# Where the nodes' scores of a four-layer graph network are computed, and when its projection runs: the scores move from TensorE to GpSimd and VectorE, the projection to another place, and one set of transposes becomes products with the identity

## The chip, the cores and the metric

The kernel runs on one core of a Trainium2 chip. The metric is the device time of one execution in microseconds (us), 1385.76 as the median of 14 runs before the change. The core has five engines that work side by side and wait for each other through semaphores: TensorE (PE, with its weight loads shown as PEld), VectorE (DVE), ScalarE (ACT), GpSimd (POOL) and SyncE (SP), which here issues nearly all DMAs. SBUF is the working memory of 128 partitions; PSUM is the small memory that matmuls write to.

## The reference, cut to what matters

x has 8 batches, 2048 nodes and 64 features. Four layers follow, each with a residual and a layer norm. Layer 0 weighs three terms of each node by the node's own weights; the second and third are products with the adjacency, A x and (2 A A - 1) x. Layer 1 projects the result and gives each node two scores per batch:

```python
    w = jnp.einsum('nd,dkio->nkio', embedding, weight)          # layer 0
    x_g = jnp.einsum('knm,bmc->bnkc', A_stack, x)
    out = jnp.einsum('bnki,nkio->bno', x_g, w)
    ...
    h = x @ W                                                   # layer 1
    s = jax.nn.leaky_relu(h @ a_node, 0.2)
    alpha = jax.nn.softmax(jnp.where(H.T > 0, s[:, None, :], NEG), axis=-1)
    agg = jnp.einsum('ben,bnf->bef', alpha, h)
    beta = jax.nn.sigmoid((h @ a_gn)[:, None, :] + (agg @ a_ge)[:, :, None])
    ...
    industry = jnp.einsum('nm,bmf->bnf', adj / deg, x @ W_ind)
```

The rest of layer 1 mixes `agg`, `h` and `industry`; layers 2 and 3 are products with the adjacency and with small weights. The change touches only how layer 0's term A x is brought into transposed form, and how and when `h`, the two scores `h @ a_node` and `h @ a_gn`, and `agg` are made.

## The kernel before, in words

The 2048 nodes are 16 tiles of 128 nodes (`NT` = 16), a tile holding 8 batches x 64 features = 512 columns. The stages are:

1. `first_product` (to about 149 us) makes y1 = A x for all tiles and keeps it as the sum of two parts, `y_hi` and `y_lo`, that TensorE can read in its rounded float32 form (fp32r).
2. `layer0` (about 150 to 743 us) is a loop over blocks j, one for each tile, and an extra round j = 16. This is where the change lies.
3. `layer1` (to about 1070 us), then layers 2 and 3.

A block of `layer0` has eight groups g = 0 to 7. In each, `weigh(j, g)` writes products of the three terms with the weights into a PSUM tile `pp` (L1020), 24 matmul instructions, and DVE adds four slices of it into the residual `r` (L1031). The PSUM pool of `pp` has two buffers. Between the groups other work of neighbouring tiles is placed, by hand: inside `program_order()` each of PE, DVE, ACT and POOL executes in exactly the order in which the Python code issues instructions, so a waiting instruction holds up all that stand behind it on its engine. SP's queue is in order too, but is arranged by the framework. The pieces that matter here:

- `first_terms(j+1)` after group 2: POOL adds `y_hi` and `y_lo` into `y1` (L956), PE transposes it (L152, named `try`), ACT copies the result to `y1T`; then the bias `bp`, and POOL prepares the next residual `r` (L969).
- `product(j+1)` after group 3: y2 = A y1 for the next tile, 32 matmuls of 512 columns (L983, `y2p`). `second_term(j+1)` after group 6: y2 transposed and finished on DVE (`y2T`, L999).
- `normed(j-1, ...)` after groups 0, 1, 2: layer norm of the tile before, ending in `x1`; `to_features(j-1)` after `product`: four transposes (`trx`), and ACT's copy `xT1`.
- `scores(j-1)` after group 6: PE multiplies `xT1` by `wa` (W times a_node and a_gn, made at the start), the tile `sgp` (L1077); ACT copies one half to `sg` and the other to `hgr`; DVE and ACT make `es` = exp(leaky_relu(score)).
- `project(j-1)` after group 7: PE multiplies `xT1` by both projections (`hp`, L1098), in a buffer of the same pool as `pp`; ACT copies `ihi` (or `y_hi`, L1115) and `h` (L1116), DVE makes `ilo` (L1117), two DMAs store `kept_i`; POOL makes `md` and `hs` = h times `es` (L1124).
- `gather(j-2)` after group 6: `aggp` accumulates `md` x `hs` (L1129).
- Masks: `mask(j+2)` (DVE, L927) from the adjacency loads, `scaled(j+1)` (POOL: `ms` L935 and sums `cs`), `compare(j+1)` (DVE, L948), `degrees(j+1)` (PE, `dgp`).

In the extra round j = 16, `gather(14)`, the sums of `es` (`denominators`, L1144), `scores(15)`, `project(15)` and `gather(15)` remain. `layer1` begins with `aggp`.

Of the kernel before, what the change touches and what calls it, by code (L numbers as in the profile page):

```python
# [8 lines left out]
F32 = mybir.dt.float32  # L9
# [9 lines left out]
P = 128  # L19
# [32 lines left out]
def kernel(  # L52
# [31 lines left out]

    ident = const.tile([P, P], F32, tag="ident", name="ident")
    make_identity(nc, ident)
    ones = const.tile([P, P], F32, tag="ones", name="ones")
    nc.vector.memset(ones, 1.0)
    eps_t = const.tile([P, 1], F32, tag="eps", name="eps_t")
# [17 lines left out]
    def b_view(t2):  # L107
        return t2.rearrange("p (b c) -> p b c", b=B)
# [771 lines left out]
    def layer0(  # L880
# [3 lines left out]

        h_sb, wb, wa, vecs, av_sb, pm, es, hgr, aggp, rden = layer1s
        raws, msk, terms, resid, norm, srow = {}, {}, {}, {}, {}, {}
        x1s, xTs, hps, hss, mds = {}, {}, {}, {}, {}

        homes = {"xT": (0, 1, 2), "xs": (3, 4), "y1": (5,), "y1T": (6, 7), "r": (8, 9),
                 "y2": (10,), "y2T": (11, 12), "cs": (13, 14), "sq": (15,)}
        turn = {}

# [7 lines left out]
        def load_adj(j):  # L902
            raws[j] = []
            for h in range(2):
                raw = rawp.tile([P, 8, P], F32, tag="raw", name=f"adj_{j}_{h}")
                for k in range(2):
                    nc.sync.dma_start(
                        raw[:, 4 * k:4 * k + 4, :],
                        at[j // 4, 2 * h + k][:, :, (j % 4) * P:(j % 4 + 1) * P],
                    )  # L910
                raws[j].append(raw)
            srow[j] = tile("srow", f"srow_{j}", (P, P), 3)
            nc.sync.dma_start(srow[j], s_row[0, j * P:(j + 1) * P].partition_broadcast(P))

        def load_x(j):
# [36 lines left out]

        def first_terms(j):

            y1 = tile("y1", f"y1_{j}")
            nc.gpsimd.tensor_tensor(y1, y_hi[:, j, :], y_lo[:, j, :], ALU.add)  # L956
            tr = ps_tr.tile([P, NP, P], F32, tag="tr", name=f"try1_{j}")
            for pr in range(NP):
                transpose(tr[:, pr, :], y1[:, pr * P:(pr + 1) * P])
            y1T = tile("y1T", f"y1T_{j}", (P, NP, P))  # L960
            nc.scalar.copy(y1T, tr)
            terms[j]["y1"] = y1T
            bp = ps_tr.tile([P, QW], F32, tag="tr", name=f"bp_{j}")
            nc.tensor.matmul(bp[:, 0:C], terms[j]["et"], bias_sb, start=True, stop=True)
            bn = tile("bn", f"bn_{j}", (P, C))
            nc.scalar.copy(bn, bp[:, 0:C])
            r = tile("r", f"r0_{j}")
            for bq in range(2):
                nc.gpsimd.tensor_tensor(  # L969
                    r[:, 4 * bq * C:4 * (bq + 1) * C]  # L970
                    .rearrange("p (h l c) -> p h l c", h=2, l=2),
                    swapped(terms[j]["xs"], bq),
                    bn.rearrange("p (h l c) -> p h l c", h=1, l=1).to_broadcast([P, 2, 2, C]),
                    ALU.add,
                )
            resid[j] = r
# [95 lines left out]
            nc.scalar.copy(xTs[j], tr)  # L1072

        def scores(j):
            sp = ps_tr.tile([P, NP, 2, 2], F32, tag="tr", name=f"sgp_{j}")
            for pr in range(NP):
                nc.tensor.matmul(  # L1077
                    sp[:, pr].rearrange("p i h -> p (i h)"), xTs[j][:, pr, :],
                    wa.rearrange("p i h -> p (i h)"), start=True, stop=True,
                )  # L1080
            sg = tile("sg", f"sg_{j}", (P, NP, 2))
            nc.scalar.copy(sg, sp[:, :, 0, :])
            nc.scalar.copy(hgr[:, j, 0, :].rearrange("p (r h) -> p r h", h=2), sp[:, :, 1, :])
            ej = es[:, j, :]
            nc.vector.scalar_tensor_tensor(
                ej.rearrange("p (r h) -> p r h", h=2), sg, 0.2, sg, op0=ALU.mult, op1=ALU.max
            )
            nc.vector.tensor_scalar(ej, ej, TOP, None, op0=ALU.min)
            nc.scalar.activation(ej, ej, AF.Exp)

        def project(j):

            mm = ps_p.tile([P, 2, 2, 4 * C], F32, tag="pp", name=f"hp_{j}")
            mm = mm.rearrange("p h l (m x) -> p h (l m) x", m=2)
            for pr in range(NP):
                for h in range(2):
                    rs = slice(h * 64, (h + 1) * 64)
                    nc.tensor.matmul(  # L1098
                        mm[:, h, pr, :], xTs[j][rs, pr, :], wb[rs], start=True, stop=True
                    )  # L1100
            if j < NT - 1:
                md = tile("md", f"md_{j}", (P, 2, E))
                nc.gpsimd.tensor_copy(md, pm[:, j, :].unsqueeze(1).to_broadcast([P, 2, E]))
                mds[j] = md.rearrange("p h e -> p (h e)")

            def by_half(t):
                return t.rearrange("p (r h c) -> p h r c", h=2, c=C)


            stay = j >= len(kept_i)  # L1110
            if stay:
                hi, lo = y_hi[:, j, :], y_lo[:, j, :]
            else:
                hi, lo = (tile(k, f"{k}_{j}", bufs=1) for k in ("ihi", "ilo"))
            nc.scalar.copy(r_(by_half(hi)), mm[:, :, :, C:2 * C])  # L1115
            nc.scalar.copy(by_half(h_sb[:, j, :]), mm[:, :, :, 0:C])  # L1116
            nc.vector.tensor_tensor(  # L1117
                r_(by_half(lo)), mm[:, :, :, C:2 * C], by_half(hi), ALU.subtract
            )
            if not stay:  # L1120
                for t, kept_part in zip((hi, lo), kept_i[j]):
                    nc.sync.dma_start(kept_part, t)
            hss[j] = tile("hs", f"hs_{j}", bufs=1)
            nc.gpsimd.tensor_tensor(  # L1124
                b_view(hss[j]), b_view(h_sb[:, j, :]), bcast(es[:, j, :]), ALU.mult
            )

        def gather(j):
            nc.tensor.matmul(aggp, mds[j], hss[j], start=j == 0, stop=j == NT - 1)  # L1129
# [1 line left out]
        def spread():  # L1131

            mds.clear()
            for q, home in enumerate((1, 2, 3, 5)):
                md = own.tile([P, 4, 2, E], F32, tag=f"b0_{home}", name=f"md4_{q}")
                nc.gpsimd.tensor_copy(
                    md, pm[:, 4 * q:4 * q + 4].unsqueeze(2).to_broadcast([P, 4, 2, E])
# [28 lines left out]
        with program_order():  # L1166
# [6 lines left out]
            for j in range(NT + 1):  # L1173
# [4 lines left out]
                for g in range(8):  # L1178
# [7 lines left out]
                    elif g == 1:  # L1186
                        when(j - 1, normed, 1)
                        if j == NT:
                            denp.append(ps_acc.tile([P, BC], F32, tag="acc", name="denp")[:, 0:B])
                            gather(NT - 2)  # L1190
                            spread()
                            denominators(0, NT - 1)
                        if first:
                            degrees(0)
                        when(j + 1, scaled, 0)
                    elif g == 2:
                        when(j - 1, normed, 2)
                        when(j + 1, first_terms)
                    elif g == 3:
                        if j + 1 < NT:  # L1200
                            for _ in product(j + 1):
                                pass
# [8 lines left out]
                        when(j + 2, mask, 1)  # L1211
                    elif g == 5:
                        when(j + 1, compare, 1)
                        if j:
                            next(flags, None)
                    elif g == 6:
                        when(j + 1, second_term)
                        when(j - 1, scores)
                        if j < NT:
                            when(j - 2, gather)  # L1220
                        else:
                            denominators(NT - 1, NT)
                            nc.vector.tensor_scalar(rden, denp[0], TINY, None, op0=ALU.max)
                            nc.vector.reciprocal(rden, rden)
                    elif g == 7:
                        when(j + 1, degrees)
                        when(j - 1, project)
            gather(NT - 1)


    def short_program(top):
# [7 lines left out]


        wb = wts.tile([P, 2 * C], F32, tag="wb", name="wb")
        wa = wts.tile([P, 2, 2], F32, tag="wa", name="wa")
        vecs = wts.tile([P, 3, C], F32, tag="vecs", name="vecs")
        pm = wts.tile([P, NT, E], F32, tag="pm", name="pm")
        es = wts.tile([P, NT, B], F32, tag="es", name="es")
# [4 lines left out]
        def load_weights():  # L1250
# [8 lines left out]
            block_diag(w2_sb[:, 1, :], w2n)  # L1259
            nc.sync.dma_start(bias2_sb, bias2.partition_broadcast(P))  # L1260
            block_diag(w3_sb, w3t)
            nc.gpsimd.memset(wa, 0.0)
            prod = wts.tile([P, C], F32, tag="prod", name="prod")
            for h in range(2):
                s = slice(h * 64, (h + 1) * 64)
                for i in range(2):
                    nc.vector.tensor_tensor(prod[s], wb[s, 0:C], vecs[s, i, :], ALU.mult)
                    nc.vector.tensor_reduce(wa[s, i, h:h + 1], prod[s], AX.X, ALU.add)

        def prepare(ps, pre):  # L1270
            for h in range(2):
# [27 lines left out]
        with tc.tile_pool(name="l0", bufs=1) as l0, tc.tile_pool(  # L1299
# [14 lines left out]
            with tc.tile_pool(name="l0s", bufs=2) as l0s, tc.tile_pool(  # L1314
# [3 lines left out]
            ) as ps_p:  # L1318
                layer0(
                    own, l0s, rawp, mskp, ps_acc, ps_tr, ps_p, w_sb, emb_sb, bias_sb, bad, deg,  # L1320
                    y_hi, y_lo, (h_sb, wb, wa, vecs, av_sb, pm, es, hgr, aggp, rden),
                )
                s1, dinv = cols_of["s1"], cols_of["dinv"]
                nc.vector.tensor_tensor(deg, deg, s1, ALU.mult)
# [717 lines left out]
```

## Time and profile before

| | before |
|---|---|
| median of 14 runs (lowest, highest) | 1385.76 us (1383.41, 1386.6) |
| the profiled execution: its own time | 1386.87 us |
| its span in the profile | 1384.8 us |
| mean TensorE clock granted | 0.96 of full |
| PE busy | 1308.0 us, 94% of the span |
| DVE busy | 929.3 us, 67% |
| ACT busy | 363.8 us, 26% |
| POOL busy | 442.5 us, 32% |

A row of the profile's groups names the source line, the engine, the operation, what it writes and reads with the shapes, and how often; then the busy time in us, the mean duration of one in ns, and the idle time of the engine just before such instructions, with what ended it. A row of a timeline begins with the start (us from the span's start) and the duration of the run of like instructions. Matmuls overlap in the pipeline, so what an instruction costs PE is read from one start to the next, not from its duration. The name behind an arrow in brackets is what the profile takes to have ended the wait; where that had long been done, it was another.

### The profile page before, as it was taken

How to read it: one execution, taken by the hardware profiler on the slowest of the kernel's cores; microseconds unless marked ns; L12 is line 12 of the kernel's file. 1: busy time of each engine (PE TensorE's matmuls, PEld its weight loads, DVE VectorE, ACT ScalarE, POOL GpSimd, SP SyncE). 2: the span in 40 equal slices, each digit the busy share in tenths (PEclk: the TensorE clock that was granted, in tenths of full speed). 3: DMA queues.
4: the chain of work that ended last, by engine and by line, in shares of the span. 5: the costliest groups of instructions: out<-in, count | busy, mean ns of one | idle time of the engine just before them, and what ended most of it. 6: DMA issues, size and time to landing. Idle time of an engine off the chain costs nothing.

```text
span 1384.8 us, 19824 instructions
## 1 busy us (share of the span) xinstructions
PE 1308.0 (94%) x7692; PEld 1025.3 (74%) x7692; DVE 929.3 (67%) x1658; ACT 363.8 (26%) x844; POOL 442.5 (32%) x372
## 2 busy tenths in 40 slices
PE   7999889999999999999986799999997899999997
PEld 6777678888888888888875466666665688888885
DVE  4555347787777777777672678888885666566554
ACT  3000101111112111111121346665655321111111
POOL 0000443444444444444410345665653320000000
PEclk9999989999999999999995699999999899999999
DMA  9765333333223332321503122222220223333552
GB/s 309 215 185 171 126 98 102 102 102 101 97 93 100 102 102 100 99 98 62 220 24 114 61 79 75 76 77 76 77 76 1 92 75 115 115 122 137 187 185 71
DMA packets 91047, 153.00 MB, mean 110 GB/s; under 512 B 12097, under 2 KB 55489, under 8 KB 84673
## 3 DMA queue, kind: packets, MB, share of 16 engines
q1 hardware_dynamic: 88642, 147.46, 31.7%
q10 hardware_dynamic: 2304, 4.20, 0.8%
q8 instruction: 63, 1.03, 0.3%
q14 instruction: 38, 0.31, 0.1%
HBM read 115.97 MB, written 35.66 MB: 110 GB/s over the span
## 4 chain that ended last, share of the span: by engine, by line
PE 91%; DVE 4%; issue 2%; ACT 1%; POOL 1%; DMA 1%; SPq 0%; POOLq 0%; ACTq 0%; DVEq 0%
PE pp L1020 24%; PE a L1288 17%; PE ind L1288 9%; PE y2p L983 9%; PE y1p L469 9%; PE fc L798 2%; PE u L1371 2%; PE df L807 2%; PE gp L693 2%; PE try L152 1%; PE yp L1400 1%; PE aggp L1129 1%; PE trm L152 1%; PE tr_l L152 1%; DVE r L1031 1%
## 5 line engine op out<-in xcount | busy, mean ns | idle before, releaser
L1031 DVE SCALAR_TENSOR_TENSOR r<-pp,emb_sb,r 128x256 f32<-128x256 f32 x512 | 247.1, 483 | 134.4 <-PE pp L1020 119.8
L1020 PE MATMUL pp<-w_sb,xT 64*128 64x256 f32 x1024 | 163.1, 391 | 11.7 <-PE hp L1098 10.3
L1020 PE MATMUL pp<-w_sb,y2T 64*128 64x256 f32 x1024 | 156.6, 378 | 0.0
L1020 PE MATMUL pp<-w_sb,y1T 64*128 64x256 f32 x1024 | 156.6, 378 | 0.0
L1020 PEld LDWEIGHTS pp<-w_sb,xT 64*128 64x128 f32 x1024 | 98.2, 187 | 34.6 <-issue 15.1
L469 PE MATMUL y1p<-x_hi,m 128*128 128x512 f32 x256 | 106.3, 415 | 7.3 <-ACT x_hi L417 7.2
L734 POOL TENSOR_TENSOR ez<-ez,coef 128x1024 f32<-128x1024 f32 x32 | 65.0, 2032 | 141.1 <-DVE ez L732 141.1
L1020 PEld LDWEIGHTS pp<-w_sb,y1T 64*128 64x128 f32 x1024 | 104.1, 188 | 7.8
L1020 PEld LDWEIGHTS pp<-w_sb,y2T 64*128 64x128 f32 x1024 | 104.1, 188 | 7.9
L1288 PE MATMUL ind<-y_hi,mj_l 128*128 128x512 f32 x256 | 106.6, 416 | 0.9 <-DVE dlt L763 0.8
L983 PE MATMUL y2p<-y_hi,msk 128*128 128x512 f32 x256 | 103.7, 405 | 0.0
L1288 PE MATMUL a<-y_hi,mj_l 128*128 128x512 f32 x256 | 102.4, 400 | 0.0
L469 PE MATMUL y1p<-x_lo,m 128*128 128x512 f32 x256 | 101.6, 397 | 0.0
L1288 PE MATMUL a<-y_lo,mj_l 128*128 128x512 f32 x256 | 101.6, 397 | 0.0
L983 PE MATMUL y2p<-y_lo,msk 128*128 128x512 f32 x256 | 101.6, 397 | 0.0
L1288 PE MATMUL ind<-y_lo,mj_l 128*128 128x512 f32 x256 | 101.0, 394 | 0.0
L1288 PE MATMUL a<-v_hi,mj_l 128*128 128x512 f32 x256 | 100.1, 392 | 0.0
L1288 PE MATMUL a<-v_lo,mj_l 128*128 128x512 f32 x256 | 100.0, 391 | 0.0
L1124 POOL TENSOR_TENSOR hs<-h,es 128x512 f32<-128x512 f32 x16 | 16.7, 1043 | 246.4 <-ACT h L1116 222.4
L935 POOL TENSOR_TENSOR ms<-msk,srow 128x1024 f32<-128x1024 f32 x32 | 77.4, 2419 | 7.5 <-DVE ms L948 5.2
L1288 PEld LDWEIGHTS ind<-y_hi,mj_l 128*128 128x128 f32 x256 | 48.6, 190 | 33.6 <-issue 19.1
L948 DVE SCALAR_TENSOR_TENSOR ms<-ms,adj 128x1024 f32<-128x1024 f32 x32 | 63.8, 1996 | 0.0
(262 smaller groups left out, 2433.3 us busy)
## 6 DMA issues: line engine op xcount, KB each, us to landing
mj_l<-mask SPq DMA_DIRECT2D x48, 1024.0 KB, 4.9
raw<-in_at SPq DMA_DIRECT2D x32, 512.0 KB, 4.9
adj<-in_at SPq DMA_DIRECT2D x64, 256.0 KB, 3.3
mask<-msk SPq DMA_DIRECT2D x32, 512.0 KB, 3.1
xraw<-in_xn SPq DMA_DIRECT2D x8, 512.0 KB, 5.5
oh<-oh SPq DMA_DIRECT2D x16, 256.0 KB, 4.1
xT<-in_xt SPq DMA_DIRECT2D x16, 256.0 KB, 2.9
xs<-in_xn SPq DMA_DIRECT2D x16, 256.0 KB, 2.5
```

Source lines behind the costliest of these rows:

```text
L152: nc.tensor.matmul(dst, src, ident, start=True, stop=True, is_transpose=True)
L469: nc.tensor.matmul(accs[q][jj], r_(m[:, t, jj * P:(jj + 1) * P]), r_(part[:, mt, :]), start=i + h + t == 0 and part is x_hi, stop=i == 3 a ...
L693: nc.tensor.matmul(gp[:, u, :], r_((oh01, oh23)[i][rs, cols]), r_(part[rs]), start=part is agg_hi, stop=part is agg_lo,)
L734: nc.gpsimd.tensor_tensor(by_b(ez), by_b(ez), per_b(coef, 2 * i, 2), ALU.mult)
L798: nc.tensor.matmul(fc[:, h, :], fcw_sb[rs], sT[rs], start=True, stop=True)
L807: nc.tensor.matmul(df[:, b:b + 1], th[:, b % 2, (b // 2) * P:(b // 2 + 1) * P], av_sb, start=True, stop=True,)
L935: nc.gpsimd.tensor_tensor(ms, m, srow[j].unsqueeze(1).to_broadcast([P, 8, P]), ALU.mult)
L948: nc.vector.scalar_tensor_tensor(ms, ms, 1.0, raws[j][h], op0=ALU.mult, op1=ALU.not_equal, accum_out=bad[:, 2 * j + h:2 * j + h + 1],)
L983: nc.tensor.matmul(acc, r_(msk[j, mt // 8][:, mt % 8, :]), r_(part[:, mt, :]), start=mt == 0 and part is y_hi, stop=mt == NT - 1 and part ...
L1020: nc.tensor.matmul(pp[:, h, pl, :], terms[j][name][rs, 2 * bq + pl], w_sb[rs, k, dq * 4 * C:(dq + 1) * 4 * C], start=k == 0, stop=k == K - 1,)
L1031: nc.vector.scalar_tensor_tensor(rb, ppv[:, :, dd, :], emb_sb[:, j, d:d + 1], rb, op0=ALU.mult, op1=ALU.add)
L1288: nc.tensor.matmul(acc, r_(a[:, mt, :]), r_(part[:, mt, :]), start=mt == 0 and part is hi, stop=mt == NT - 1 and part is lo,)
```

## The change

Three things, all in `layer0`, and what follows from them:

- `scores` uses no matmul any more. In `project`, POOL multiplies `h` by a_node and by a_gn into `hs` and a new tile `hm`; `scores` sums each over the features on DVE; a new `scale_h` on POOL then overwrites `hs` with `h` times `es`. `wa` and its making disappear.
- The order: `project(j-2)` stands after group 3, ahead of `product(j+1)`; `scores(j-2)` after group 5; `scale_h(j-2)` after group 6; `gather(j-2)` after group 7, behind `degrees`. In the extra round the last two tiles are finished one after the other.
- `first_terms` makes y1's transposed form by eight fp32r matmuls with an fp32r copy of the identity, `y_hi` and `y_lo` accumulating in PSUM; POOL's sum of the two disappears.

`srow` has two buffers in place of three.

```diff
@@ setup
+    ident_r = const.tile([P, P], F32, tag="ident_r", name="ident_r")
+    nc.vector.tensor_copy(r_(ident_r), ident)
@@ layer0
-        homes = {"xT": (0, 1, 2), "xs": (3, 4), "y1": (5,), "y1T": (6, 7), "r": (8, 9),
+        homes = {"xT": (0, 1, 2), "xs": (3, 4), "hs": (5,), "y1T": (6, 7), "r": (8, 9),
                  "y2": (10,), "y2T": (11, 12), "cs": (13, 14), "sq": (15,)}
...
-            srow[j] = tile("srow", f"srow_{j}", (P, P), 3)
+            srow[j] = tile("srow", f"srow_{j}", (P, P))
...
         def first_terms(j):
-            y1 = tile("y1", f"y1_{j}")
-            nc.gpsimd.tensor_tensor(y1, y_hi[:, j, :], y_lo[:, j, :], ALU.add)
             tr = ps_tr.tile([P, NP, P], F32, tag="tr", name=f"try1_{j}")
             for pr in range(NP):
-                transpose(tr[:, pr, :], y1[:, pr * P:(pr + 1) * P])
+                for part in (y_hi, y_lo):
+                    nc.tensor.matmul(
+                        tr[:, pr, :], r_(part[:, j, pr * P:(pr + 1) * P]), r_(ident_r),
+                        start=part is y_hi, stop=part is y_lo,
+                    )
...
         def scores(j):
-            sp = ps_tr.tile([P, NP, 2, 2], F32, tag="tr", name=f"sgp_{j}")
-            for pr in range(NP):
-                nc.tensor.matmul(
-                    sp[:, pr].rearrange("p i h -> p (i h)"), xTs[j][:, pr, :],
-                    wa.rearrange("p i h -> p (i h)"), start=True, stop=True,
-                )
-            sg = tile("sg", f"sg_{j}", (P, NP, 2))
-            nc.scalar.copy(sg, sp[:, :, 0, :])
-            nc.scalar.copy(hgr[:, j, 0, :].rearrange("p (r h) -> p r h", h=2), sp[:, :, 1, :])
             ej = es[:, j, :]
-            nc.vector.scalar_tensor_tensor(
-                ej.rearrange("p (r h) -> p r h", h=2), sg, 0.2, sg, op0=ALU.mult, op1=ALU.max
-            )
+            sg = tile("sg", f"sg_{j}", (P, B))
+            nc.vector.tensor_reduce(sg, b_view(hss[j]), AX.X, ALU.add)
+            nc.vector.scalar_tensor_tensor(ej, sg, 0.2, sg, op0=ALU.mult, op1=ALU.max)
             nc.vector.tensor_scalar(ej, ej, TOP, None, op0=ALU.min)
             nc.scalar.activation(ej, ej, AF.Exp)
+            nc.vector.tensor_reduce(hgr[:, j, 0, :], b_view(hms[j]), AX.X, ALU.add)
+
+        def scale_h(j):
+            nc.gpsimd.tensor_tensor(
+                b_view(hss[j]), b_view(h_sb[:, j, :]), bcast(es[:, j, :]), ALU.mult
+            )
...
         def project(j):
...
-            hss[j] = tile("hs", f"hs_{j}", bufs=1)
-            nc.gpsimd.tensor_tensor(
-                b_view(hss[j]), b_view(h_sb[:, j, :]), bcast(es[:, j, :]), ALU.mult
-            )
+            hss[j], hms[j] = (tile(k, f"{k}_{j}", bufs=1) for k in ("hs", "hm"))
+            for i, t in enumerate((hss[j], hms[j])):
+                nc.gpsimd.tensor_tensor(
+                    b_view(t), b_view(h_sb[:, j, :]),
+                    vecs[:, i, :].unsqueeze(1).to_broadcast([P, B, C]), ALU.mult,
+                )
...
                     elif g == 1:
                         when(j - 1, normed, 1)
                         if j == NT:
...
-                            gather(NT - 2)
                             spread()
-                            denominators(0, NT - 1)
+                            denominators(0, NT - 2)
...
                     elif g == 3:
+                        when(j - 2, project)
                         if j + 1 < NT:
                             for _ in product(j + 1):
                                 pass
...
                     elif g == 5:
                         when(j + 1, compare, 1)
+                        when(j - 2, scores)
...
                     elif g == 6:
                         when(j + 1, second_term)
-                        when(j - 1, scores)
+                        when(j - 2, scale_h)
+                    elif g == 7:
+                        when(j + 1, degrees)
                         if j < NT:
                             when(j - 2, gather)
-                        else:
-                            denominators(NT - 1, NT)
-                            nc.vector.tensor_scalar(rden, denp[0], TINY, None, op0=ALU.max)
-                            nc.vector.reciprocal(rden, rden)
-                    elif g == 7:
-                        when(j + 1, degrees)
-                        when(j - 1, project)
+            denominators(NT - 2, NT - 1)
+            gather(NT - 2)
+            project(NT - 1)
+            scores(NT - 1)
+            scale_h(NT - 1)
+            denominators(NT - 1, NT)
+            nc.vector.tensor_scalar(rden, denp[0], TINY, None, op0=ALU.max)
+            nc.vector.reciprocal(rden, rden)
             gather(NT - 1)
@@ short_program: wa, and the products and sums that made it at the start, are removed
```

More of the change, by code (lines that the diff above doesn't have):

```diff
@@ L883, in layer0 @@
     ):
-        h_sb, wb, wa, vecs, av_sb, pm, es, hgr, aggp, rden = layer1s
+        h_sb, wb, vecs, av_sb, pm, es, hgr, aggp, rden = layer1s
         raws, msk, terms, resid, norm, srow = {}, {}, {}, {}, {}, {}
-        x1s, xTs, hps, hss, mds = {}, {}, {}, {}, {}
-        homes = {"xT": (0, 1, 2), "xs": (3, 4), "y1": (5,), "y1T": (6, 7), "r": (8, 9),
+        x1s, xTs, hms, hss, mds = {}, {}, {}, {}, {}
+        homes = {"xT": (0, 1, 2), "xs": (3, 4), "hs": (5,), "y1T": (6, 7), "r": (8, 9),
                  "y2": (10,), "y2T": (11, 12), "cs": (13, 14), "sq": (15,)}
@@ L1100, in project @@
                     )
-            if j < NT - 1:
+            if j not in mds:
                 md = tile("md", f"md_{j}", (P, 2, E))
@@ L1133, in spread @@
             mds.clear()
-            for q, home in enumerate((1, 2, 3, 5)):
+            for q, home in enumerate((1, 2, 3, 10)):
                 md = own.tile([P, 4, 2, E], F32, tag=f"b0_{home}", name=f"md4_{q}")
@@ L1241, in short_program @@
         wb = wts.tile([P, 2 * C], F32, tag="wb", name="wb")
-        wa = wts.tile([P, 2, 2], F32, tag="wa", name="wa")
         vecs = wts.tile([P, 3, C], F32, tag="vecs", name="vecs")
@@ L1261, in load_weights @@
             block_diag(w3_sb, w3t)
[L1262 to L1268, printed above, removed]
         def prepare(ps, pre):
@@ L1320, in short_program @@
                     own, l0s, rawp, mskp, ps_acc, ps_tr, ps_p, w_sb, emb_sb, bias_sb, bad, deg,
-                    y_hi, y_lo, (h_sb, wb, wa, vecs, av_sb, pm, es, hgr, aggp, rden),
+                    y_hi, y_lo, (h_sb, wb, vecs, av_sb, pm, es, hgr, aggp, rden),
                 )
```

## The prediction

> **What bounds the kernel now.** I read the page first (engine shares, chain), then the waits of the layer-0 stretch, then one block of 128 nodes on each engine's timeline, then the two ends of the stage.
>
> ```profile
> PE 1308.0 (94%) x7692; PEld 1025.3 (74%) x7692; DVE 929.3 (67%) x1658; ACT 363.8 (26%) x844; POOL 442.5 (32%) x372
> ...
> PE 91%; DVE 4%; issue 2%; ACT 1%; POOL 1%; DMA 1%; SPq 0%; POOLq 0%; ACTq 0%; DVEq 0%
> ...
> L1020 PE MATMUL pp<-w_sb,xT 64*128 64x256 f32 x1024 | 163.1, 391 | 11.7 <-PE hp L1098 10.3
> ```
>
> The chain that ended last is PE in 91% of its length, so what PE is given to do, or waits for, is paid. Layer 0 runs from 150 to 743 us in blocks of 35.1 us; in the window 531.5 to 566.6 PE is busy 34.31 us, DVE 26.57, POOL 15.91, ACT 6.92. The idle column of the third line holds the only regular PE wait: 10.3 us, in 13 blocks. The PE timeline of that block, from y2's transposes to the next block's first group:
>
> ```profile
> 547.41 0.66 PE L152 MATMUL try<-ident,y 128*128 128x128 f32 x4
> 547.90 0.95 PE L1077 MATMUL sgp<-wa,xT 128*128 128x4 f32 x8
> 548.71 1.10 PE L1129 MATMUL aggp<-hs,md 128*128 128x512 f32 x2
> 549.75 0.70 PE L1020 MATMUL pp<-w_sb,xT 64*128 64x256 f32 x4
> ...
> 552.85 1.16 PE L1098 MATMUL hp<-wb,xT 64*128 64x128 f32 x16
> 554.80 0.70 PE L1020 MATMUL pp<-w_sb,xT 64*128 64x256 f32 x4 [0.79 <-PE hp L1098]
> ```
>
> Read start to start: the scores' eight products hold PE 547.90 to 548.71, **0.81 us**; the projection holds it 552.85 to 554.80, **1.95 us**, the last 0.79 idle. That wait is named PE hp, but hp had long ended. The next group needs a PSUM buffer of the pair that the group before hp filled, and DVE empties that one only at 554.7 (its last `r` instructions run 552.66 to 554.70). One extra user of the pair, with too little PE work behind it, makes the wait.
>
> The second place is block 0. PE timeline, then GpSimd's:
>
> ```profile
> 172.04 0.60 PE L1020 MATMUL pp<-w_sb,y2T 64*128 64x256 f32 x4
> 177.42 1.11 PE L152 MATMUL try<-ident,y 128*128 128x128 f32 x4 [4.79 <-POOL y L956]
> 178.47 0.68 PE L964 MATMUL bp<-bias_sb,et 16*128 16x64 f32 x2
> 179.08 1.23 PE L1020 MATMUL pp<-w_sb,xT 64*128 64x256 f32 x4
> ```
>
> ```profile
> 170.33 3.27 POOL L935 TENSOR_TENSOR ms<-msk,srow 128x1024 f32<-128x1024 f32 x1 [5.25 <-DVE ms L948]
> ...
> 176.11 1.26 POOL L956 TENSOR_TENSOR y<-y_hi,y_lo 128x512 f32<-128x512 f32 x1
> ```
>
> y1's sum waits on GpSimd behind the mask products, and those for a DVE compare: PE stands still 4.79 us. The group after it takes 5.42 us (179.08 to 184.50) where it normally takes 2.60, since the clock was granted at half.
>
> [...] after the 4.79 us, rows of 0.60 take 1.06. [...] sgp's eight matmuls have only 4 columns each, so loads set their pace, and they start every 0.10 us (0.81 / 8). [...] compare (L948) takes 2.94 us at 533.54 beside a GpSimd product, 1.14 us at 546.89 alone.
>
> **The change part by part**, in blocks whose order on each engine I read from the two programs.
>
> *Scores off PE.* sgp goes: -0.81 in 15 blocks = **-12.2**. The work returns elsewhere: two GpSimd products per block (the nearest row, he<-agg,vecs, took 1.26; so 2.5), less y1's sum (1.27); on DVE two reductions of 128x512 (0.68 as s_l) = 1.4; ACT loses two copies (0.17 each). Covers: GpSimd 15.9+1.25 of 34, DVE 26.6+1.4 = 28 of 34, so neither total binds; the order is looked at below.
>
> *Projection before y2's product.* hp (about 1.05 of PE) stays, but behind it stand 7.5 us of y2p and a transpose, in which DVE empties the buffer. So -(1.95-1.05) = -0.90 in about 14 blocks = **-12.6**. In block 15 there is no y2p: +0.5 there. Its evacuation (two ACT copies, DVE's ilo 0.69) and compare and masks (2.9 each) follow group 3 on DVE: done about 9.0 us after group 3, and group 4 ends at 11.9, so 2.9 us stay spare. The two `kept_i` stores move ahead of `srow` and adj loads on SP's queue; they wait for ilo, ready at +3.1, while srow waits for GpSimd's mask product (about +7) anyway, and the loads are for the next block's masks. On GpSimd the two products wait for ACT's h (about +2.4) and hold the mask product behind them to about +7.5; who waits for that is compare at group 5, at +16.5. The third srow buffer goes: its load then waits for a product that SP already waited for. Both at nothing; without that cover a load would be up to 4 us late against some 20 us of slack.
>
> *y1 by identity products.* Four transposes (527.73 to 528.32, 0.59, and 0.1 of wait on GpSimd's y) become eight fp32r products with a full weight load each. No such run exists in the trace. From below: the lone fp32r product of 128 columns, sm (L390), lets the next matmul start 0.06 us later: 8 x 0.06 = 0.48, a gain of 0.1. From above: 0.228 as for 512 columns, 1.82, a loss of 1.2. I take sgp's load pace [...] so with edges +0.3 in 16 blocks = **+4.8** (ends -1.6 and +19). Block 0's wait disappears, and with it the half clock: -4.79 - (5.42-2.60) = **-7.6**. Late next there: the y2 product's masks, ready since 151, so nothing.
>
> *The chain that the new scores hang on.* From the start S of DVE's group 5: group 1.96, compare 1.14, reduction 0.71, two small steps 0.36, Exp 0.3 (table loaded early, ACT is free), scale_h on GpSimd 1.04: done at S+5.55. PE comes to gather, now after degrees, at S-0.2 + groups 6 and 7 (5.3) + y2's transposes 0.5 + 0.3 = S+5.9. So gather waits for nothing, with **0.4 us to spare**; behind it stand all next groups. Group 6 leaves DVE at S+6.9, PE needs its buffer at S+7.0 after gather (1.04); group 7 at 9.4 against 9.6. Tight, and DVE is then level with PE until group 3 (DVE could end at S+20.2, PE's group 3 ends at S+18.7 and its DVE part at +20.7). I add 0.1 per block for brushes: **+1.5**.
>
> *The end of layer 0.* Before, from the last group at 719.84 to the last gather's end at 742.69: 22.9 us. After, in order: gather 13 and 28 denominators to +6.7, hp 14 to +8.7 (half clock, as hp at 736.24 took 2.08), trx; ACT h +10.0, GpSimd product +11.1, reduction, two steps, Exp +12.5, scale_h +13.6, gather 14 +15.7, hp 15 +17.8, h +19.0, product +20.1, reduction to Exp +21.5, scale_h +22.6, gather +24.7. With the products at 1.26, +25.1: **+2** (0 if the clock stays whole, +4 if the waits stretch).
>
> The ident_r copy on DVE lies in the 3.8 us that it waits for the first load; the removed weight products for `wa` are some small DVE steps. Nothing.
>
> Sum: -12.2 -12.6 +0.5 +4.8 -7.6 +1.5 +2 = **-23.6 us**. The profiled execution took 1386.87 (span 1384.8 and 2.1 around it), so 1363.3; it stood 1.1 above the median of 1385.76, so **1362.2**.
>
> **Rivals.**
> - *fp32r products at the price of 512 columns* (1.82 a block): -23.6 + 14.7 = -9, **1377**. For: no run of them in the trace. Against: sm's 0.06.
> - *The gather chain is late* (ends slower). It decides from 0.4 us on, then 1:1 on PE, 14 times. If compare at group 5 runs in its 2.94 us form (GpSimd's two extra products push its mask work beside it) and scale_h doubles beside DVE, the chain is 2.8 late: 2.4 x 14 = 34, and DVE's level stretch after it adds about 0.5 x 14 = 7: +17, **1403**. With compare alone slow: 1.4 x 14 = 20, **1382**. Against: GpSimd's mask work should end 11.7 us after group 3, compare comes at 16.5.
> - *The gain is absorbed*: DVE's level stretch stalls PE 1.4 us a block, and only block 0's part, the end and little else remain: **1382 to 1385**. Against: each buffer check above is met.
>
> **How the numbers follow.** Forecast 0.80 (own range 1355 to 1371: fp32r price down to 0.06, end 0 to +4, brushes 0 to 0.4 a block), fp32r dear 0.08, chain late 0.07 (0.05 of it slower), absorbed 0.05 (half under 1383). A run of this kernel tells apart some 0.2%, 2.8 us. Faster 0.91, same 0.03, slower 0.06. Range 1354 to 1378: it takes in the dear products and leaves out the late chain, the absorbed gain and the tails of the forecast, together under 2 in 10.
>
> **What would show it.** Right: no PE wait named hp; the y1 products in place of the try wait near 172 us, and pp at 0.60 behind them; blocks of about 33.7 us; PE aggp without idle time; last gather some 2 us later after the last group. Wrong: PE aggp waiting for POOL hs, pp waiting for DVE r in groups 0 to 2, y1 products starting 0.2 us apart, or blocks still at 35.

## The result, and the profile after

| | before | after |
|---|---|---|
| median (lowest, highest) | 1385.83 us (1383.41, 1388.45) of 28 runs | 1367.45 us (1366.96, 1406.6) of 6 runs |
| the profiled execution: its own time | 1386.87 us | 1365.25 us |
| its span | 1384.8 us | 1363.5 us |
| PE, DVE, POOL busy in the profile | 1308.0, 929.3, 442.5 us | 1294.6, 956.6, 463.0 us |
| from y2's product of tile 2 to that of tile 15, start to start | 456.06 us | 446.33 us |

The ratio is 0.9865, with a 95% interval from 0.9855 to 0.9876: 18.4 us less by the medians, where 23.6 had been forecast. The execution of 1406.6 us was disturbed and is left out of the ratio. The lines of layer 0 have moved by two to four: `pp` is L1024, `r` L1035, `y2p` L987, `hp` L1100, `aggp` L1133, the transposes L154.

The page after, with the lines that answer to those of before:

```profile
PE 1294.6 (95%) x7628; PEld 1011.8 (74%) x7628; DVE 956.6 (70%) x1683; ACT 358.3 (26%) x810; POOL 463.0 (34%) x386
...
L1024 PE MATMUL pp<-w_sb,xT 64*128 64x256 f32 x1024 | 161.7, 391 | 9.4 <-issue 6.9
```

No wait is named hp any more. But the idle column has only gone from 11.7 to 9.4 us: other waits stand there, and for 6.9 us of them the profile names no releaser ("issue"). They come from a few blocks. A late block, from which they are absent, on PE's timeline:

```profile
501.73 0.66 PE L154 MATMUL try<-ident,y 128*128 128x128 f32 x4
502.31 0.70 PE L1024 MATMUL pp<-w_sb,xT 64*128 64x256 f32 x4
...
505.10 0.38 PE L1009 MATMUL dgp<-ones,cs 128*128 128x1 f32 x2
505.35 1.10 PE L1133 MATMUL aggp<-hs,md 128*128 128x512 f32 x2
506.38 0.70 PE L1024 MATMUL pp<-w_sb,xT 64*128 64x256 f32 x4
...
514.35 0.33 PE L960 MATMUL try<-ident_r,y_hi 128*128 128x128 f32 x1
514.52 0.28 PE L960 MATMUL try<-ident_r,y_lo 128*128 128x128 f32 x1
...
515.19 0.27 PE L960 MATMUL try<-ident_r,y_lo 128*128 128x128 f32 x1
515.39 0.43 PE L968 MATMUL bp<-bias_sb,et 16*128 16x64 f32 x2
...
518.45 1.06 PE L1100 MATMUL hp<-wb,xT 64*128 64x128 f32 x16
```

No row has a bracket. The scores' products are gone, `gather` comes behind `degrees` without a wait, and such a block takes 33.65 us where it took 35.07. Over one block's length, from 493.80 to 527.45, PE is busy for the whole time (33.65 of 33.65 us), DVE for 28.08 (forecast 28).

The same timeline in block 0, where PE had stood still for 4.79 us:

```profile
172.14 0.33 PE L960 MATMUL try<-ident_r,y_hi 128*128 128x128 f32 x1
...
173.54 0.70 PE L1024 MATMUL pp<-w_sb,xT 64*128 64x256 f32 x4
174.07 0.60 PE L1024 MATMUL pp<-w_sb,y1T 64*128 64x256 f32 x4
```

Neither the wait nor the half clock is left: the granted clock is 1.00 from 172.14 to 177.00, where before it was 0.50 from 177.00 to 184.50.

**What the forecast had not seen.** Start to start, the y2 products of tiles 2 to 8 are 32.93, 34.14, 35.21, 36.45, 37.83 and 34.24 us apart; only from tile 8 on is it 33.65. Against 33.65 the last five of these, which hold groups 4 to 7 of blocks 2 to 6, lose 9.6 us in sum. In blocks 1 to 7, group 5, a generator `lists_flag` issues one step of a test of the inputs, a few small DVE instructions and in block 6 also a product on PE (`next(flags)`, in group 5 after the change as before). In block 4, PE's, DVE's and GpSimd's timelines of the changed kernel read:

```profile
329.54 1.10 PE L1133 MATMUL aggp<-hs,md 128*128 128x512 f32 x2
333.37 0.70 PE L1024 MATMUL pp<-w_sb,xT 64*128 64x256 f32 x4 [2.72 <-issue]
```

```profile
328.14 0.89 DVE L248 TENSOR_SCALAR flagbox<-flagbox 128x16 f32<-128x16 f32 x1
329.06 0.17 DVE L249 TENSOR_REDUCE flagbox<-flagbox 128x1 f32<-128x16 f32 x1
329.15 2.16 DVE L250 SCALAR_TENSOR_TENSOR flagbox<-av_sb 128x1 f32<-128x1 f32 x1
331.24 2.03 DVE L1035 SCALAR_TENSOR_TENSOR r<-pp,emb_sb,r 128x256 f32<-128x256 f32 x4
```

```profile
327.96 1.04 POOL L1089 TENSOR_TENSOR hs<-h,es 128x512 f32<-128x512 f32 x1 [6.78 <-ACT es L1085]
328.96 2.34 POOL L937 TENSOR_TENSOR ms<-msk,srow 128x1024 f32<-128x1024 f32 x1
```

The first of these instructions and the last had these lines in the kernel before:

```profile
336.80 0.17 DVE L246 TENSOR_SCALAR flagbox<-flagbox 128x16 f32<-128x16 f32 x1
337.09 0.15 DVE L248 SCALAR_TENSOR_TENSOR flagbox<-av_sb 128x1 f32<-128x1 f32 x1
```

L250 works on one element per partition, took 0.15 us before, and takes 2.16 us here. It ends at 331.31; GpSimd's mask product ends at 331.30. L248 (0.17 us before, 0.89 here) ends at 329.03, and `scale_h` at 329.00. So each stood on DVE until the GpSimd instruction that had begun before it was done. The `r` of group 6 is behind them on DVE and ends at 333.27, and PE, which needs the buffer that they empty, begins the next group at 333.37. In block 5 L258 does the same (0.15 us before, 1.96 here), and in block 2 L242 (0.18 before, 0.68 here). Their ends agree with GpSimd's too: L258 ends at 367.76 and the mask product of its block at 367.76, L242 at 259.67 and `scale_h` at 259.63. Before, GpSimd ran nothing beside the same steps of block 4 (no instruction from 334 to 340 us). L250 and L258 have two inputs in SBUF, L248 and L242 have one, and the reduction L249, which also has one, isn't held: 0.17 us beside the mask product, 0.17 before. What sets the held instructions apart isn't shown.

Two of the five losses are of another kind. In block 3 the step is one reduction, which is not held (1.90 us before):

```profile
292.93 1.93 DVE L244 TENSOR_REDUCE flagbox<-pm 128x64 f32<-128x1024 f32 x1
```

It takes 1.9 us of DVE wherever it stands (1.93 in experiment 1, 1.91 in experiment 2), and PE loses 1.56. In block 6 no flag step is held, and the loss is not new: that stretch was 0.83 us longer than its neighbours before the change and is 0.60 longer after it. So the change added 8.8 us in these blocks (9.6 less 0.83).

### The profile page after: what moved, and what is told of

The parts are those of the page before. It is cut to its first block, busy times and chain, and to the rows that moved or that the text cites. A ratio compares the mean times of both kernels' runs of the same rounds, so it can differ in the third digit from the quotient of the medians.

```text
span 1363.5 us, 19744 instructions
## 1 busy us (share of the span) xinstructions
PE 1294.6 (95%) x7628; PEld 1011.8 (74%) x7628; DVE 956.6 (70%) x1683; ACT 358.3 (26%) x810; POOL 463.0 (34%) x386
## 4 chain that ended last, share of the span: by engine, by line
PE 81%; DVE 4%; issue 2%; ACT 1%; POOL 1%; ACTq 0%; DVEq 0%; POOLq 0%
PE pp L1024 24%; PE a L1288 17%; PE ind L1288 9%; PE y2p L987 9%; PE fc L800 2%; PE u L1371 2%; PE df L809 2%; PE gp L695 2%; DVE r L1035 1%; PE yp L1400 1%; PE try L960 1%; PE aggp L1133 1%; PE trm L154 1%; PE tr_l L154 1%; PE red L745 1%
## 5 line engine op out<-in xcount | busy, mean ns | idle before, releaser
L1035 DVE SCALAR_TENSOR_TENSOR r<-pp,emb_sb,r 128x256 f32<-128x256 f32 x512 | 247.1, 483 | 94.4 <-PE pp L1024 80.5
L1024 PE MATMUL pp<-w_sb,xT 64*128 64x256 f32 x1024 | 161.7, 391 | 9.4 <-issue 6.9
L1024 PE MATMUL pp<-w_sb,y2T 64*128 64x256 f32 x1024 | 154.9, 377 | 0.0
L1024 PE MATMUL pp<-w_sb,y1T 64*128 64x256 f32 x1024 | 154.9, 377 | 0.0
L973 POOL TENSOR_TENSOR r<-xs,bn 128x256 f32<-128x256 f32 x32 | 22.5, 725 | 297.7 <-ACT bn L970 149.2
L1024 PEld LDWEIGHTS pp<-w_sb,xT 64*128 64x128 f32 x1024 | 95.8, 187 | 34.0 <-issue 22.8
L1024 PEld LDWEIGHTS pp<-w_sb,y1T 64*128 64x128 f32 x1024 | 101.5, 188 | 9.7
L1024 PEld LDWEIGHTS pp<-w_sb,y2T 64*128 64x128 f32 x1024 | 101.4, 188 | 9.8
L987 PE MATMUL y2p<-y_hi,msk 128*128 128x512 f32 x256 | 103.6, 405 | 0.0
L987 PE MATMUL y2p<-y_lo,msk 128*128 128x512 f32 x256 | 101.7, 397 | 0.0
L937 POOL TENSOR_TENSOR ms<-msk,srow 128x1024 f32<-128x1024 f32 x32 | 82.4, 2574 | 5.5 <-DVE ms L950 5.5
L929 DVE TENSOR_SCALAR msk<-adj 128x1024 fp32r<-128x1024 f32 x32 | 63.8, 2027 | 4.1 <-PE y1p L471 4.1
```

Source lines behind the costliest of these rows:

```text
L929: nc.vector.tensor_scalar(r_(m), raws[j][h], 0.0, None, op0=ALU.is_gt)
L937: nc.gpsimd.tensor_tensor(ms, m, srow[j].unsqueeze(1).to_broadcast([P, 8, P]), ALU.mult)
L987: nc.tensor.matmul(acc, r_(msk[j, mt // 8][:, mt % 8, :]), r_(part[:, mt, :]), start=mt == 0 and part is y_hi, stop=mt == NT - 1 and part ...
L1024: nc.tensor.matmul(pp[:, h, pl, :], terms[j][name][rs, 2 * bq + pl], w_sb[rs, k, dq * 4 * C:(dq + 1) * 4 * C], start=k == 0, stop=k == K - 1,)
L1035: nc.vector.scalar_tensor_tensor(rb, ppv[:, :, dd, :], emb_sb[:, j, d:d + 1], rb, op0=ALU.mult, op1=ALU.add)
```

## The experiments

"Flag steps" are those of `lists_flag`. A *pitch* is the time from the start of one y2 product to the next.

**1. The flag steps at another place.** The changed kernel, in the main loop:

```diff
                     elif g == 3:
 ...
+                        if j:
+                            next(flags, None)
 ...
                     elif g == 5:
 ...
-                        if j:
-                            next(flags, None)
```

> The changed kernel with one edit: the flag steps of blocks 1 to 7 (some small DVE instructions and a DMA each) are issued at the end of group 3 instead of in group 5 behind the scores. Theory (the flag steps lie in the stretch in which DVE is level with TensorE, and some of them stand still on DVE until a GpSimd product ends): the blocks of 34.1 to 37.8 us in the changed kernel (five of them, 9.7 us above 33.65 in sum) come back to about 33.7, so 8 to 9.7 us less: about 1358 to 1359.5. Rival (the longer blocks come from another cause, such as a late transposed x or a DMA): blocks 3 to 5 stay at 35 to 38 us and the time stays at 1367.

Measured: 1355.53 us, 11.9 less than the changed kernel; ratio to before 0.9755 (0.970 to 0.981). The pitches from tile 3 on are 33.64 to 33.83. The profiled execution took longer, 1371.16 us: its last gather ends at 713.56, 9.4 ahead of the changed kernel's 722.98, but in layer 1 the granted clock was lower (0.92 against 0.98 between 850 and 950 us). So only its layer 0 is read. DVE's timeline in block 4:

```profile
317.44 0.66 DVE L250 SCALAR_TENSOR_TENSOR flagbox<-av_sb 128x1 f32<-128x1 f32 x1
318.81 0.48 DVE L1035 SCALAR_TENSOR_TENSOR r<-pp,emb_sb,r 128x256 f32<-128x256 f32 x1 [0.71 <-PE pp L1024]
```

L250 is held again, 0.66 in place of 0.15 (it ends at 318.10, the GpSimd sum beside it, L942, at 318.08), but DVE then waits 0.71 us for PE: the hold fits into slack. The theory holds for the place of the steps. The medians regain 2 us more than it expected; in the trace layer 0 ends 9.4 us earlier, and where the rest lies is not shown. This run alone can't tell a hold from plain DVE time.

**2. Is it the hold, or only DVE time in a tight stretch?** The changed kernel, the two neighbours in group 5 exchanged:

```diff
-                        when(j - 2, scores)
                         if j:
                             next(flags, None)
+                        when(j - 2, scores)
```

> The changed kernel with one edit: in group 5 the flag steps stand ahead of the scores' steps on DVE, not behind them, so that they do not run beside GpSimd's scale_h and mask product. They stay in the same stretch of DVE. Theory (most of the 9.7 us come from small DVE steps that stand still until a running GpSimd product ends): the steps cost 0.15 to 0.9 us again, the flag blocks come down by half or more, about 1361 to 1362. Rival (the mere DVE time of the flag steps in a stretch without slack is the cost, wherever it stands there): the blocks stay at 35 to 38 us, 1366 to 1368.

Measured: 1359.29 us, 8.2 less than the changed kernel; ratio to before 0.9808 (0.9795 to 0.9821). DVE's timeline in block 4, then a line of PE's in block 3:

```profile
327.69 0.17 DVE L248 TENSOR_SCALAR flagbox<-flagbox 128x16 f32<-128x16 f32 x1
...
327.98 0.15 DVE L250 SCALAR_TENSOR_TENSOR flagbox<-av_sb 128x1 f32<-128x1 f32 x1
```

```profile
296.82 1.12 PE L1133 MATMUL aggp<-hs,md 128*128 128x512 f32 x2 [1.19 <-POOL hs L1089]
```

The instructions are the same and the stretch of DVE is the same, but GpSimd is idle there (for 7.13 us up to 329.45), and they cost 0.15 to 0.17 us again. The stretches of blocks 2, 4 and 5 come down from 34.14, 36.45 and 37.83 us to 33.66, 33.73 and 33.90, 7.1 us in sum. So the hold was most of the loss. Block 6 stays at 34.25, and block 3 hardly moves: 35.16 in place of 35.21. Its reduction of 1.9 us (L244) made `r` late behind the scores; now ahead of them it makes their chain late, and `gather` waits 1.19 us for `hs`. For this block the rival is right: 1.9 us of DVE cost about 1.5 at either place. The chain's small slack is real; that is the forecast's late-chain rival, at one place.

**3. The projection alone.** The kernel before:

```diff
                     elif g == 3:
+                        if j < NT:
+                            when(j - 2, project)
 ...
                     elif g == 7:
 ...
-                        when(j - 1, project)
+                        if j == NT:
+                            project(NT - 1)
```

with `project(NT - 2)` at group 1 of the extra round.

> The kernel before with the projection alone moved: project(j-2) behind group 3, ahead of y2's product; scores stay matmuls, y1 stays a GpSimd sum with transposes. In the extra round project(14) stands at group 1 and project(15) at group 7. Theory of the prediction: 0.90 us less in about 14 blocks, 12.6 in sum, blocks of 34.2 instead of 35.1 us, no wait of pp named hp: about 1373. Rival (the wait only moves to another group of the block): blocks stay at 35.1 and the time at 1385.

Measured: 1376.49 us, 9.2 less than its before; ratio 0.9924 (0.990 to 0.9949). The group row on its page:

```profile
L1020 PE MATMUL pp<-w_sb,xT 64*128 64x256 f32 x1024 | 161.4, 392 | 1.7 <-DVE r L1031 1.7
```

The hp wait of 10.3 us is gone, and the pitch is 33.99, 1.08 less, more than forecast: 14.4 less from y2's product of tile 1 to that of tile 15 (487.24 to 472.84). The total moved only 9.2, because from there to the last gather's end it lost 6.3 (70.95 to 77.21). PE's timeline there:

```profile
705.42 1.06 PE L1098 MATMUL hp<-wb,xT 64*128 64x128 f32 x16
713.62 2.08 PE L1129 MATMUL aggp<-hs,md 128*128 128x512 f32 x2 [7.14 <-POOL hs L1124]
```

That is this variant's own order: ACT's copy of `h` stands behind tile 15's layer norm and runs at 711.86. The steady part bears the theory out; the end is no evidence for the changed kernel, which has another order there.

**4. The changed kernel with the projection late.** `when(j - 2, project)` is taken out of group 3, and `when(j - 1, project)` stands behind `gather` in group 7.

> The changed kernel with the projection alone back at the end of the block (project(j-1) behind gather and group 7; its products with a_node and a_gn then start earlier, the rest stays). Theory: the wait of the next group for the buffer of pp comes back, 0.9 us in 14 blocks: about 1380, blocks of 34.5 us. Rival (the wait went because the scores' matmuls went, not because of the projection's place): within 2 us of 1367.

Measured: 1387.26 us, 19.8 more than the changed kernel, and no different from before: ratio 1.0003 (0.9984 to 1.0022). The pitch is 35.02, so the projection's place is worth 1.37 a block here, not 0.9. PE's timeline, then DVE's:

```profile
518.62 1.16 PE L1100 MATMUL hp<-wb,xT 64*128 64x128 f32 x16
520.87 0.70 PE L1024 MATMUL pp<-w_sb,xT 64*128 64x256 f32 x4 [1.09 <-issue]
```

```profile
518.73 2.03 DVE L1035 SCALAR_TENSOR_TENSOR r<-pp,emb_sb,r 128x256 f32<-128x256 f32 x4
```

`hp` takes 2.25 us of PE, of which 1.09 is a wait for the buffer that the `r` row empties at 520.76. Before, that wait was 0.79. The two reductions of the new scores stand ahead of those rows on DVE and make the buffer later: DVE works without a pause from 513.45 on, where in the block of before it still waited 1.72 us for PE ahead of that row. So the rival is out, and the size was missed: scores on DVE need the projection elsewhere.

**5. y1's products alone, for all tiles.** The kernel before with the diff's `ident_r`, its `first_terms` and two `srow` buffers.

> The kernel before with y1's transposed form alone made by the identity products (with the fp32r copy of the identity and two srow buffers). Theory: block 0 gives 7.6 to 8.2 us back (no wait for GpSimd's sum, no half clock), the other blocks cost 0.3 to 0.45 us each, 5 to 6.5 in sum: 1 to 3 us less, about 1384. Rival (the products cost what the other matmuls hide): 8 us less, 1378. Rival (fp32r products dear): 1388 or more.

Measured: 1383.2 us, 2.5 less; ratio 0.9969 (0.9943 to 0.9995). y2's product of tile 1 begins 24.16 us after tile 0's, in place of 31.66: 7.5 less. Every steady pitch is 35.50 in place of 35.07: 0.43 more. That is the theory.

**6. The same for tiles 0 and 1 only.** The edit is shown against experiment 5's kernel:

```diff
+                if j >= 2:
+                    transpose(tr[:, pr, :], y1[:, pr * P:(pr + 1) * P])
+                    continue
                 for part in (y_hi, y_lo):
```

and the sum by GpSimd likewise from j = 2 on.

> The kernel before with y1's identity products for tiles 0 and 1 only, all others by GpSimd's sum and four transposes as before. Theory: block 0 gives 7.3 us back as when all tiles use the products, and the 0.43 us that each later block paid goes: about 1378. Rival (the products' price in later blocks is hidden or part of it lies elsewhere): 1383 as with all tiles.

Measured: 1376.81 us, 9.2 less than its before (1386.05); ratio 0.9934 (0.992 to 0.9948). Pitches are back at 35.06, and block 0's gain stays. Of the 16 tiles the products pay for the first two only; the gain stands in block 0, where tile 1's are made.

**7. Both remedies.** The changed kernel with the edits of experiments 1 and 6; `y1` takes turns with `hs` in one place of SBUF.

> The changed kernel with the flag steps at the end of group 3, and y1's identity products for tiles 0 and 1 only; from tile 2 on y1 is again GpSimd's sum and four transposes (its tile takes turns with hs). Theory: the flags' 11 us and 14 times 0.43 us, 6 in sum: about 1350. Rival (GpSimd's sum comes late behind the new products, or a mask product is pushed into DVE's level stretch): 1355 to 1360, with a try wait named POOL y.

Measured: **1348.78 us**, 18.7 less than the changed kernel; ratio to before 0.9727 (0.9714 to 0.974). No `try` wait is named POOL y. The windows of one block (us, then the busy time and number of instructions of each engine):

```profile
473.20:506.40 33.20, 33.20 (x260) 27.43 (x258) 28.15 (x51) 6.69 (x12) 18.32 (x17) 1.00 0.32 106
```

The pitch is 33.20, 0.45 less than after the change, with PE still busy throughout and GpSimd 1.25 us busier (18.32 against 17.07), which nothing waits for. It beats both kernels.

## Why the prediction was right, point by point

| step | forecast | measured |
|---|---|---|
| scores off PE | -0.81 a block | -0.77, by difference: -1.42 + 1.08 - 0.43 |
| the projection ahead of y2's product | -0.90 a block | -1.08 with the scores still on PE, -1.37 with them on DVE |
| y1 by identity products | +0.3 a block | +0.43 alone, +0.45 in the changed kernel |
| block 0 | -7.6, +0.3 for the products | -7.5 (experiment 5) |
| brushes (small late arrivals) | +0.1 a block | none in blocks without flag steps |
| flag steps | not in the sum | +8.8 in the trace, +11.9 by the medians of experiment 1 |
| from the last group to the last gather's end | +2 | 23.2 us in place of 22.85: +0.4 |

- **The bound, the cover and the direction** were right: PE carries the time, and scores, wait and block 0 gave what their rows said. The steady pitch was forecast as about 33.7 and is 33.65.
- **The gather chain** was worked out within 0.2 us (its terms add up to S+5.51, not 5.55). In the block shown, `scale_h` ends at 504.80 and PE comes at 505.35: 0.55 to spare, forecast 0.4. The cover is real but thin: 1.9 us of DVE ahead of the scores used it up in experiment 2.
- **The fp32r products** begin 0.11 us apart, close to the 0.10 of the `sgp` products whose pace the forecast took; there the eight weight loads fill 547.79 to 548.76. From that pace the +0.3 is 0.81 less the transposes' 0.59, and an estimate for the edges. The eight took 1.04 us (514.35 to 515.39), 0.45 more than the transposes, because the first pair costs 0.17 and the step to `bp` 0.20. The rival with dear products is out.
- **The step that failed** is the term "I add 0.1 per block for brushes". The sentence ahead of it, "DVE is then level with PE until group 3", was right, but the term asked what the new work does to that stretch, and not what old work already stood in it. The flag steps were in group 5 before too, where DVE had slack; the change did not move one of them. It filled the slack around them and put GpSimd's `scale_h`, with the mask product behind it, beside them. The forecast had the price at hand: it had read `compare` at 2.94 us beside a GpSimd product and at 1.14 alone. It applied that to the large instructions and left out the small ones. So the third rival, a gain absorbed by DVE's stretch, came true in four blocks: in blocks 2, 4 and 5 by the hold, which it did not name, and in block 3 by DVE time, which it did. With the flag steps elsewhere (experiment 1) the gain is 30.2 us by the medians.
- **The projection was undersized**: by 0.18 alone, some 2.5 us in 14 blocks, and by 0.47 in company. The forecast took the wait of before; once the scores are on DVE the wait it avoids is longer. The effects of two edits were added as if each were alone. Experiment 4 shows the difference. The two rows can't both be read at their best: beside -1.37 the scores are worth only -0.48 by the same difference. The pair gave -1.85 a block, where -1.71 was forecast.
- **The end of layer 0** was oversized. PE's timeline after:

```profile
699.76 1.12 PE L1133 MATMUL aggp<-hs,md 128*128 128x512 f32 x2
700.73 3.22 PE L1148 MATMUL denp<-es,md 128*128 128x8 f32 x28
703.88 2.08 PE L1100 MATMUL hp<-wb,xT 64*128 64x128 f32 x16
...
719.77 0.60 PE L1148 MATMUL denp<-es,md 128*128 128x8 f32 x2 [4.22 <-ACT es L1085]
720.89 2.08 PE L1133 MATMUL aggp<-hs,md 128*128 128x512 f32 x2 [0.52 <-POOL hs L1089]
```

  The 28 denominators now hold PE for 3.15 us (700.73 to 703.88) and have no wait ahead of them; before, behind a wait of 2.29, 30 of them took 6.02. The forecast had kept their old duration, and that was one at a lower clock: 0.52 was granted between 724.2 and 730.2 before, 0.98 between 700.7 and 703.9 after. The projections do run at half clock (2.08; 0.50 was granted from 703.88 to 706.00), as forecast, and the serial chain shows as the wait of 4.22.
- **In sum** the range held because two errors lay on opposite sides: the flag steps, which cost 11.9 us by the medians of experiment 1 and had no term, and the other terms, which together came out 6.6 us better than forecast. That the forecast came within 5.2 us of the median is partly luck. Some 1.6 us of the shorter span lie behind layer 0 (642.1 against 640.5 from the last gather's end), which the change does not touch; they are not explained by any step.

## What to carry to other kernels

When a change takes the slack out of a stretch of an engine, list everything that is issued there, old and small instructions too, and move away what can run elsewhere: here a few small instructions that nobody had moved cost 9 to 12 of some 30 us. The DVE instructions that were held here took what was left of the GpSimd instruction beside them, whatever their own size (2.16 us for one of 0.15, 0.89 for one of 0.17), and 0.15 to 0.17 us where GpSimd was idle: place such instructions there, or where DVE has slack. Where a rewrite cures one block's wait (y1's products in block 0), use it in that block alone.

## What the runs showed of the hardware

- A DVE instruction of one element per partition took 2.16 us beside a GpSimd product and 0.15 alone. The profile shows the hold as a longer busy time of DVE, and PE's wait behind it as "issue"; no row names GpSimd.
- It is not all of DVE: a reduction of 128x16 (L249) that began at 329.06, with GpSimd's mask product already running, took its usual 0.17 us. The instructions held had one SBUF input (L248) or two (L250, L258).
- The same wait did not always cost clock. After 2.72 us idle in block 4 the next row took 0.70 us, at a granted clock of 1.00; after 2.72 us in block 5 the granted clock was 0.50 from 369.8 to 372.5, and PE's timeline has:

```profile
369.82 1.22 PE L1024 MATMUL pp<-w_sb,xT 64*128 64x256 f32 x4 [2.72 <-issue]
...
372.51 0.68 PE L1024 MATMUL pp<-w_sb,xT 64*128 64x256 f32 x4
```

  The half clock lasted for 2.7 us and made that block the longest, 37.83 us. What sets the two waits apart isn't shown.
